# A gated recurrent layer on one core: VectorE's order within a step, and the x products dealt out anew

## The chip, the cores and the metric

The kernel runs on one core of a Trainium2 chip. The metric is the device time of one execution in microseconds (us). The kernel before took 1719.35 us, the median of three runs (1719.15 to 1720.79).

## The reference

The input x has 8 sequences of 512 steps with 512 features, all float32. A state h (8 x 512) starts from `cond_1024` and is carried through the steps:

```
fused = sigmoid(concat([x_t, h]) @ w_W + w_b)      # 1024 columns
r, z  = split(fused, 2)
m     = x_t @ wx_W + wx_b + r * (h @ wh_W + wh_b)
h_new = z * h + (1 - z) * tanh(m)
```

The output is x plus the sequence of the h_new. What depends on h alone must be done step after step; what depends on x (three products of 512 x 512 per step) can be done ahead.

## The kernel before, in words

**Layout.** Features stand on partitions. A step's products with h use h as the stationary operand (32 columns: four steps of 8 sequences, three of them zero) and weights as the moving one. TensorE is used as four column strips of 32: each product is four matmuls (j = 0 to 3, line 343) that write four groups of 32 partitions side by side. One such matmul shows as two records in the profile, so a product is 8 records. The result is transposed 32 x 32 by VectorE, so that features stand on partitions again.

**Halves and banks.** The state is in two halves, A (features of k = 0, 1) and B (k = 2, 3); the names in the profile say it (hTA, hTB, md0A, hd0B). The results of one step go to three PSUM tiles: bank A of 192 columns (h, z, r of half A), bank B of 128 (r, h of half B) and bank C of 64 (z of half B). "h" in this list is the product with `wh_W`.

**Order on TensorE** (line 32, loop at 337): A0 B0 A1 A2 A3 B1 B2 B3 C0 C1 C2 C3, a bank and the k of the state that it reads. A0 and A1 need the two quarters of the new half A, A2 and A3 those of the new half B. Behind the twelve come a few x products of later steps (lines 346 to 349). They are taken from a generator, `products` (line 289): for each eight steps (an octet, two groups of four) seven products in the manner of Winograd, each of two k and 192 columns, into four regions AL, DE, BE, GA of the PSUM tiles xp. That makes 14 products of one k, 56 matmuls. `take(later, 8 if s else 4)` takes one product in the first step of a group of four, and two in the others. From step 5 to step 500 there are such products; the first five steps do three larger, plain ones, and the last eleven none.

**The step on VectorE and ScalarE** (lines 420 to 445), written out by hand: the schedule is manual, so each engine runs its instructions in this order.
- `turn_r(0)`: VectorE transposes r of half A out of bank A (tr, line 371), ScalarE takes its sigmoid into md0A.
- `turn_h(0)`: VectorE transposes h into md1A (line 386).
- `turn_z(0)`: VectorE transposes z (tz, line 371); ScalarE takes the sigmoid of its negative into hd0A. A dependency made by hand (line 395) lets tz wait for r's sigmoid.
- `memory(0, q)` for the two quarters: a scan on VectorE (line 355) makes m = r * h + the x part from md0A and md1A; ScalarE takes tanh.
- `turn_r(1)`: the same for half B, out of bank B.
- `update(0, 0)`: a scan (line 355) makes the first quarter of the new half A, hTA.
- `turn_h(1)`, `turn_z(1)`, then `update(0, 1)`, which waits by hand for r's sigmoid of half B (line 429).
- `memory(1, q)`, `update(1, q)`: the same for half B.

Behind these come, spread over the octet (lines 444 to 501), ScalarE's copies of the new state, copies and additions that prepare PSUM and read the finished x products (lines 250 to 255 and 452 to 492), three small memsets on VectorE (line 499), and GpSimd's additions for the output (line 501) and for the x products (line 287). SyncE loads x and stores the output by chunks of 16 steps.

Of the kernel before, what the change touches and what calls it, by code (L numbers as in the profile page):

```python
# [14 lines left out]
NQ = 4  # L15
# [9 lines left out]
SYNC = mybir.DependencyInfo(mybir.DependencyClass.Sync, mybir.DependencyReason.DATA)  # L25
# [7 lines left out]
HALF = 192  # L33
# [8 lines left out]
def tile_cond_rnn_residual(  # L42
# [144 lines left out]
    def mm(out_, lhsT, rhs, start=False):  # L187
        nc.tensor.matmul(  # L188
            out_, lhsT, rhs, start=start, stop=False, skip_group_check=True
        )  # L190
# [23 lines left out]
    def act(key, out_, in_, func, **kw):  # L214
        inst = nc.scalar.activation(out_, in_, func, **kw).ins  # L215
        if key in written:
            tc.declare_no_dep(inst, written[key], reason="ordered through VectorE")
        written[key] = inst
        return inst
# [37 lines left out]
    def reg(r):  # L257
        return xps[r[0]][:, r[1]]

    def wx_of(kh, ch):  # L260
        return wx[:, 2 * kh : 2 * kh + 2, :, HALF * ch : HALF * ch + HALF]

    def x_half(o, n, kh):

        return x_of(o // 2, slice(2 * kh, 2 * kh + 2), 8 * (o % 2) + GS * n, GS)
# [23 lines left out]
    def products(o):  # L289

        t_ = [q[o % 2] for q in sx]
        for to, lhs, rhs in (
            (AL, x_half(o, 0, 0), wx_of(0, 0)),
            (DE, t_[0], tw[0]),
            (BE, t_[1], tw[1]),
            (AL, x_half(o, 0, 1), wx_of(1, 0)),
            (GA, t_[2], tw[2]),
            (BE, t_[3], wx_of(1, 1)),
            (GA, x_half(o, 1, 1), tw[3]),
        ):  # L300
            for k in range(2):
                for j in range(NQ):
                    mm(reg(to)[32 * j : 32 * j + 32], lhs[:, k], rhs[:, k, j])
                    yield

    def take(it, n=None):
        while n is None or n > 0:
            if next(it, it) is it:
                return
            n = None if n is None else n - 1  # L310

    def x_side():
        for o in range(2, NG // 2):
            yield from products(o)
# [4 lines left out]
    later = x_side()  # L319
# [8 lines left out]
    for i in range(T):  # L328
        g, s = divmod(i, GS)
# [7 lines left out]
        for n in (ORDER if i else FIRST).split():  # L337
# [3 lines left out]
            bank, k = n[0], int(n[1])  # L341
            hs = hT[k // 2][i % NH][:, :, k % 2, 2]
            for j in range(NQ):
                to = ps[bank] if i or bank != "A" else xps[0][:, XP["A"]]
                mm(to[32 * j : 32 * j + 32, :], hs, wh(bank, k, j))
        if i < 5:
            take(first[(i + 3) // 2], 2)
        else:
            take(later, 8 if s else 4)

        rows = slice(B * s, B * s + B)

        def scan(c_, out_, d0, d1):

            return nc.vector.tensor_tensor_scan(  # L355
                *[t_[:, :, c_].rearrange("p n c s -> p (n c s)") for t_ in (out_, d0, d1)],
                0.0,
                ALU.mult,
                ALU.add,
            ).ins  # L360
# [8 lines left out]
        def turned(n, hf):  # L369
            t_ = work.tile([P, 2, 32], F32, tag=f"t{n}{hf}", name=f"t{n}{hf}_{i}")  # L370
            inst = nc.vector.transpose(t_.rearrange("p c n -> p (c n)"), raw[n][hf]).ins  # L371
            return t_[:, :, rows], inst

        r_done = [None, None]

        def turn_r(hf):
            tr, _ = turned("r", hf)
            r_done[hf] = act(
                ("r", hf, g % 2, s),
                md0[hf][g % 2][:, rows, :, 1].rearrange("p n c -> p c n"),  # L380
                tr,
                AF.Sigmoid,
            )

        def turn_h(hf):
            inst = nc.vector.transpose(
                md1[hf][g % 2][:, :, :, 0].rearrange("p n c -> p c n"), raw["h"][hf]
            ).ins
            if hf == 0 and i + 1 - NH in pool_done:
                tc.add_manual_dep(inst, pool_done[i + 1 - NH].name, SYNC)  # L390

        def turn_z(hf):
            tz, inst = turned("z", hf)
            if hf == 0:
                tc.add_manual_dep(inst, r_done[0].name, SYNC)
            act(
                ("zc", hf, i % 2),
                hd0[hf][i % 2][:, :, :, 2].rearrange("p n c -> p c n"),
                tz,
                AF.Sigmoid,  # L400
                scale=-1.0,
            )
# [6 lines left out]
        def memory(hf, q):  # L409

            c_ = slice(q, q + 1)
            scan(c_, ms[hf], md0[hf][g % 2][:, rows], md1[hf][g % 2][:, rows])
            act(("n", hf, q, i % NH), state(hf, i, 1)[:, :, c_], ms[hf][:, :, c_, 1], AF.Tanh)

        def update(hf, q):
            s1 = (i + 1) % GS
            new = hT[hf][(i + 1) % NH][:, B * s1 : B * s1 + B]
            return scan(slice(q, q + 1), new, hd0[hf][i % 2], hT[hf][i % NH][:, rows])

        turn_r(0)  # L420
        turn_h(0)
        turn_z(0)
        memory(0, 0)
        memory(0, 1)
        turn_r(1)
        update(0, 0)
        turn_h(1)
        turn_z(1)
        tc.add_manual_dep(update(0, 1), r_done[1].name, SYNC)
        if i == 0:  # L430
# [169 lines left out]
```

## Time and profile before

| what | value |
|---|---|
| median of 3 runs | 1719.35 us |
| profiled execution | 1723.04 us, its span 1720.5 us |
| TensorE (PE), matmuls | 1698.3 us busy, 99% of the span |
| TensorE (PEld), weight loads | 1414.3 us busy, 82% |
| VectorE (DVE) | 1126.3 us busy, 65% |
| ScalarE (ACT) | 959.0 us busy, 56% |
| GpSimd (POOL) | 303.1 us busy, 18% |
| granted TensorE clock | 1.000 |

How to read it: matmuls are pipelined and their ends are modelled, so 99% does not say that TensorE works all the time; weight loads overlap the matmuls. The helpers record most instructions under one line each: all matmuls are line 188, all sigmoids, tanhs and state copies line 215, all scans line 355. The tiles tell them apart: out<-in. In a timeline the columns are the start (us from the span's start), the length from the first start to the last end, engine, line, operation, tiles and shapes, how many, and in brackets the engine's idle time before it with what ended it. In the waits view they are who waits, for whom, the total in us, how often, and the longest.

### The profile page before, as it was taken

To read this page: it belongs to the slowest core of one execution; us is meant where nothing else is said; L and a number is where in the kernel's file an instruction comes from. 1 tells how busy PE (TensorE), PEld (TensorE's weight loads), DVE (VectorE), ACT (ScalarE), POOL (GpSimd) and SP (SyncE) were. 2 spreads that over 40 slices of the span, in tenths; PEclk is the share of its full clock that TensorE was granted. 3 is DMA by queue.
4 is the path that set the end of the run, shared out by engine and by line. 5 is a ranking of instruction groups with operands and counts; after the bars stand their busy time and mean duration, and the time that the engine had idled before them with its cause. 6 is when DMAs were issued, how large, how long until landed. Compare 5 with 4: busy or idle time off the path is not lost.

```text
span 1720.5 us, 129875 instructions
## 1 busy us (share of the span) xinstructions
PE 1698.3 (99%) x56238; PEld 1414.3 (82%) x56238; DVE 1126.3 (65%) x9387; ACT 959.0 (56%) x5822; POOL 303.1 (18%) x1281
## 2 busy tenths in 40 slices
PE   9999999999999999999999999999999999999998
PEld 5888888888888888888888888888888888888886
DVE  5666666666666666666666666666666666666665
ACT  3555555555555555555555555555555555555554
POOL 1111111111111111111111111111111111111111
PEclk9999999999999999999999999999999999999999
DMA  4000000000000000000000000000000000000000
GB/s 174 17 5 17 17 17 17 17 5 17 17 17 17 5 17 17 17 17 5 17 17 17 18 11 11 17 17 17 17 5 17 17 18 17 5 17 11 11 11 10
DMA packets 11525, 31.40 MB, mean 18 GB/s; under 512 B 1220, under 2 KB 1732, under 8 KB 10824
## 3 DMA queue, kind: packets, MB, share of 16 engines
q1 hardware_dynamic: 10800, 22.94, 3.8%
q8 instruction: 440, 7.21, 1.7%
q14 instruction: 133, 1.09, 0.2%
q10 hardware_dynamic: 152, 0.16, 0.0%
HBM read 14.70 MB, written 8.39 MB: 13 GB/s over the span
## 4 chain that ended last, share of the span: by engine, by line
PE 88%; DVE 6%; ACT 4%; issue 1%; DMA 0%
PE A L188 42%; PE B L188 21%; PE xp L188 15%; PE C L188 10%; DVE tz L371 2%; DVE tr L371 2%; ACT md0A L215 2%; ACT hd0A L215 2%; DVE hTA L355 2%; ACT hTA L215 1%; DMA rows<-in_bias_dram 0%; DVE bias L203 0%; ACT hTB L215 0%; ACT xp L223 0%; DVE rows L120 0%
## 5 line engine op out<-in xcount | busy, mean ns | idle before, releaser
L188 PE MATMUL A<-wa,hTA 128*32 128x192 f32 x8176 | 527.3, 329 | 13.3 <-DVE hTA L355 4.0
L188 PE MATMUL A<-wa,hTB 128*32 128x192 f32 x8176 | 446.2, 335 | 0.2 <-DVE hTB L355 0.2
L188 PE MATMUL B<-wb,hTA 128*32 128x128 f32 x8192 | 414.0, 273 | 0.0
L501 POOL TENSOR_TENSOR ot<-xin,hTB 128x16 f32<-128x16 f32 x503 | 125.5, 250 | 1371.0 <-DVE hTB L355 1359.6
L371 DVE STREAM_TRANSPOSE tr<-A 128x64 f32<-128x64 f32 x511 | 127.9, 250 | 358.7 <-PE A L188 358.7
L188 PEld LDWEIGHTS A<-wa,hTB 128*32 128x32 f32 x8176 | 243.6, 125 | 111.5 <-DVE hTB L355 92.3
L188 PEld LDWEIGHTS B<-wb,hTA 128*32 128x32 f32 x8192 | 292.8, 121 | 40.9
L188 PEld LDWEIGHTS A<-wa,hTA 128*32 128x32 f32 x8176 | 236.2, 123 | 109.4 <-DVE hTA L355 61.6
L188 PE MATMUL B<-wb,hTB 128*32 128x128 f32 x8192 | 318.7, 273 | 0.0
L215 ACT ACTIVATE md0A<-tr 128x16 f32<-128x16 f32 x512 | 112.9, 221 | 318.2 <-DVE tr L371 318.2
L188 PEld LDWEIGHTS B<-wb,hTB 128*32 128x32 f32 x8192 | 241.4, 122 | 0.0
L355 DVE TENSOR_TENSOR_SCAN hTB<-hd0B,hTB 128x24 f32<-128x24 f32 x1024 | 158.1, 196 | 100.2 <-ACT hTB L215 100.0
L355 DVE TENSOR_TENSOR_SCAN hTA<-hd0A,hTA 128x24 f32<-128x24 f32 x1024 | 191.9, 187 | 43.1
L215 ACT ACTIVATE hd0B<-tz 128x16 f32<-128x16 f32 x512 | 115.7, 226 | 175.8 <-DVE tz L371 175.8
L188 PE MATMUL C<-wb,hTA 128*32 128x64 f32 x8192 | 209.4, 219 | 0.0
L188 PE MATMUL C<-wb,hTB 128*32 128x64 f32 x8192 | 209.3, 219 | 0.0
L215 ACT ACTIVATE hd0A<-tz 128x16 f32<-128x16 f32 x512 | 116.0, 227 | 162.0 <-DVE tz L371 162.0
L188 PEld LDWEIGHTS C<-wb,hTA 128*32 128x32 f32 x8192 | 186.9, 122 | 0.0
L371 DVE STREAM_TRANSPOSE tz<-A 128x64 f32<-128x64 f32 x511 | 128.0, 251 | 79.0 <-ACT md0A L215 75.9
L188 PE MATMUL xp<-tw,sx 128*32 128x192 f32 x2976 | 168.2, 326 | 0.1
L215 ACT ACTIVATE hTB<-hTB 128x16 f32<-128x16 f32 x512 | 121.8, 238 | 79.8 <-DVE hTB L355 75.5
L215 ACT ACTIVATE hTB<-m 128x8 f32<-128x8 f32 x1024 | 160.8, 206 | 0.0
(91 smaller groups left out, 2292.0 us busy)
## 6 DMA issues: line engine op xcount, KB each, us to landing
xin<-in_x_dram SPq DMA_DIRECT2D x31, 256.0 KB, 3.3
out_dram<-ot SPq DMA_DIRECT2D x31, 256.0 KB, 2.2
wx<-in_wx_dram SPq DMA_DIRECT2D x4, 768.0 KB, 7.1
wa<-in_wa_dram SPq DMA_DIRECT2D x4, 384.0 KB, 9.0
wb<-in_wb_dram SPq DMA_DIRECT2D x1, 1152.0 KB
wb<-in_wb_dram SPq DMA_DIRECT2D x1, 384.0 KB, 11.1
out_dram<-ot SPq DMA_DIRECT2D x1, 192.0 KB, 3.6
head<-in_xh_dram ACTq DMA_DIRECT2D x1, 144.0 KB, 5.1
```

The costliest lines, as they stand in the source:

```text
L188: nc.tensor.matmul(out_, lhsT, rhs, start=start, stop=False, skip_group_check=True)
L215: inst = nc.scalar.activation(out_, in_, func, **kw).ins
L355: return nc.vector.tensor_tensor_scan(*[t_[:, :, c_].rearrange("p n c s -> p (n c s)") for t_ in (out_, d0, d1)], 0.0, ALU.mult, ALU.add,).ins
L371: inst = nc.vector.transpose(t_.rearrange("p c n -> p (c n)"), raw[n][hf]).ins
L501: return engine.tensor_tensor(ot[:, t, 2 * hf : 2 * hf + 2, :].rearrange("p c n -> p n c"), x_of(c, slice(2 * hf, 2 * hf + 2), t, 1).rearr ...
```

## The change

Three things are edited.
1. tz of half A no longer waits by hand for r's sigmoid, but for the transpose of h ahead of it on VectorE. The wait for r's sigmoid is then with the scan that reads it.
2. On VectorE, the transpose of h of half B stands ahead of the first update of half A, no longer behind it.
3. Each step takes 8 matmuls from the generator. To make the number come out, 2 of the 14 products of one k in an octet are each done as two of 96 columns: 64 matmuls for eight steps. The x columns of four steps in a row, from the first of a group, were 192, 384, 384, 384; they are now 384, 384, 288, 288.

```diff
     def products(o):
...
-        for to, lhs, rhs in (
+        for n, (to, lhs, rhs) in enumerate((
             (AL, x_half(o, 0, 0), wx_of(0, 0)),
             (DE, t_[0], tw[0]),
             (BE, t_[1], tw[1]),
...
             (GA, t_[2], tw[2]),
             (BE, t_[3], wx_of(1, 1)),
             (GA, x_half(o, 1, 1), tw[3]),
-        ):
+        )):
             for k in range(2):
-                for j in range(NQ):
-                    mm(reg(to)[32 * j : 32 * j + 32], lhs[:, k], rhs[:, k, j])
-                    yield
+                w = HALF // 2 if (2 * n + k) % 7 == 3 else HALF
+                for c0 in range(0, HALF, w):
+                    for j in range(NQ):
+                        mm(
+                            reg(to)[32 * j : 32 * j + 32, c0 : c0 + w],
+                            lhs[:, k],
+                            rhs[:, k, j, c0 : c0 + w],
+                        )
+                        yield
...
-            take(later, 8 if s else 4)
+            take(later, 8)
...
         r_done = [None, None]
+        h_done = [None, None]
...
             inst = nc.vector.transpose(
                 md1[hf][g % 2][:, :, :, 0].rearrange("p n c -> p c n"), raw["h"][hf]
             ).ins
+            h_done[hf] = inst
...
             if hf == 0:
-                tc.add_manual_dep(inst, r_done[0].name, SYNC)
+                tc.add_manual_dep(inst, h_done[0].name, SYNC)
...
         turn_r(1)
+        turn_h(1)
         update(0, 0)
-        turn_h(1)
         turn_z(1)
```

## The prediction

> **What bounds the kernel now.** I read the chain of work that ended last, then the waits, then the timeline of single steps. By the chain's own engines the kernel looks bound by TensorE:
>
> ```profile
> PE 88%; DVE 6%; ACT 4%; issue 1%; DMA 0%
> ```
>
> The waits view speaks against that. TensorE's weight loads wait for VectorE's state of half B in nearly every step, and for half A in a quarter of them:
>
> ```profile
> PEld A L188 <- DVE hTB L355: 92.3, 499, 0.6
> DVE tz L371 <- ACT md0A L215: 76.0, 491, 0.2
> PEld A L188 <- DVE hTA L355: 61.6, 136, 0.6
> ```
>
> The test is a step with no x product. VectorE's timeline of such a step near the end, from its r transpose of half A to the next:
>
> ```profile
> 1698.71 0.25 DVE L371 STREAM_TRANSPOSE tr<-A 128x64 f32<-128x64 f32 x1 [0.76 <-PE A L188]
> 1698.89 0.21 DVE L386 STREAM_TRANSPOSE md1A<-A 128x64 f32<-128x64 f32 x1
> 1699.25 0.25 DVE L371 STREAM_TRANSPOSE tz<-A 128x64 f32<-128x64 f32 x1 [0.15 <-ACT md0A L215]
> 1699.42 0.23 DVE L355 TENSOR_TENSOR_SCAN m<-md0A,md1A 128x16 f32<-128x16 f32 x2
> 1699.57 0.23 DVE L371 STREAM_TRANSPOSE tr<-B 128x64 f32<-128x64 f32 x1
> 1699.88 0.21 DVE L355 TENSOR_TENSOR_SCAN hTA<-hd0A,hTA 128x24 f32<-128x24 f32 x1
> 1700.01 0.23 DVE L386 STREAM_TRANSPOSE md1B<-B 128x64 f32<-128x64 f32 x1
> 1700.15 0.21 DVE L371 STREAM_TRANSPOSE tz<-C 128x64 f32<-128x64 f32 x1
> ...
> 1700.81 0.31 DVE L355 TENSOR_TENSOR_SCAN hTB<-hd0B,hTB 128x24 f32<-128x24 f32 x2 [0.19 <-ACT hTB L215]
> ...
> 1702.01 0.25 DVE L371 STREAM_TRANSPOSE tr<-A 128x64 f32<-128x64 f32 x1 [0.76 <-PE A L188]
> ```
>
> It lasts 3.30 us. The 496 steps with x products go from the tr row at 39.55 to the one at 1682.20: 1642.65 / 496 = 3.31 us, the regular ones 3.306 (some 3 us sit in a few stragglers). Taking all x work away thus buys nothing: the period is that of a loop through VectorE. TensorE's and ScalarE's rows of the same step close it:
>
> ```profile
> 1700.14 0.55 PE L188 MATMUL A<-wa,hTA 128*32 128x192 f32 x8 [0.40 <-DVE hTA L355]
> 1700.73 0.51 PE L188 MATMUL A<-wa,hTA 128*32 128x192 f32 x8
> 1701.07 0.88 PE L188 MATMUL A<-wa,hTB 128*32 128x192 f32 x16
> ```
>
> ```profile
> 1698.99 0.22 ACT L215 ACTIVATE md0A<-tr 128x16 f32<-128x16 f32 x1 [0.80 <-DVE tr L371]
> 1699.53 0.22 ACT L215 ACTIVATE hd0A<-tz 128x16 f32<-128x16 f32 x1 [0.32 <-DVE tz L371]
> 1699.65 0.30 ACT L215 ACTIVATE hTA<-m 128x8 f32<-128x8 f32 x2
> ```
>
> The **B loop**: tr at 1698.71, first update of half B ends at 1700.81+0.21 = 1701.02, A2 starts at 1701.07 (2.36 after tr), next tr 0.94 later: 3.30. The **A loop**: the update ends at 1700.09, A0 starts at 1700.14 (1.43 after tr). A late A0 takes 0.59 to A1 (1700.14 to 1700.73); from there an early step, in which nothing waits, gives 0.33 to A2 and 0.90 from A2 to tr (27.82): 1.43+0.59+0.33+0.90 = 3.25. **TensorE's own** time comes from the same early step:
>
> ```profile
> 26.59 0.51 PE L188 MATMUL A<-wa,hTA 128*32 128x192 f32 x8
> 26.92 0.83 PE L188 MATMUL A<-wa,hTB 128*32 128x192 f32 x16
> ...
> 28.67 1.47 PE L188 MATMUL xp<-wx,xin 128*32 128x384 f32 x16
> ```
>
> A0 starts at 26.05 and x at 28.67: 2.62 for the twelve state products. One 192-column x product takes 0.325 (rows at 802.34, 802.66, 802.99), so steps with 384 columns need 3.27 and those with 192 need 2.95. The period is the largest of the three: 3.30, B, always.
>
> **The change, part by part.**
>
> *z transpose of half A (tz).* Its wait for r's sigmoid becomes a wait for h's transpose, which stands just ahead of it on VectorE. Behind it queue the A scans, tr of B and all that follows. Today tz starts 0.04 after the sigmoid's end (1698.99+0.22 = 1699.21, tz 1699.25). h ends at 1698.89+0.21 = 1699.10. No row shows VectorE waiting for itself. Bounds: tz at 1699.07 if the wait costs nothing beyond the engine's spacing (0.18, tr to h); at 1699.17 if it costs the 0.07 between the last A matmul's recorded end (801.42) and tr (801.49). I take 0.03 to 0.04, the usual step between VectorE and ScalarE: 1699.13, so 0.12 earlier, by the rows nearest in kind.
>
> *r's sigmoid at the scan.* It ends at 1699.21, the result is there by 1699.25; behind tz the scan issues at 1699.13+0.17 = 1699.30. The wait is covered by tz, with 0.05 to spare. The tanh then follows z's sigmoid by 0.12 as now, and m is ready in time (0.16 after the scan's start, against 0.40 to the tanh less the 0.17). So A's update moves 0.12 earlier: A0 can start 1.31 after tr, and the A loop is 3.13.
> The Trainium skill, "Perfetto Trace Analysis", section "Identifying Dependency Chains", speaks against this step: an instruction that waits for several engines may get a semaphore instruction ahead of it, and the scan now needs ScalarE's r and VectorE's h. The waits view shows the pattern of today, tz waiting for ScalarE and the scan for nobody; after, tz waits for h and the scan for r, so the rule should find one wait on each. By the rule the scan would be late by a price the page does not give.
> I bound such a price from rows: nothing, or 0.04 as for any handover; of this 0.04 would stay within the A loop, 3.17.
>
> *h of half B ahead of A's update.* It needs bank B, as tr of B ahead of it does. Moved up, it issues 0.17 after tr of B (now 1699.57, then 1699.45): 1699.62, and frees VectorE 0.13 later, at 1699.75. A's update is due at 1699.76. It fits in the hole of 0.31 that VectorE leaves today between 1699.57 and 1699.88. If that cover is short, A's update pays what is missing, up to 0.05. Behind the update nothing but tz of B stands: it starts at 1699.76+0.13 = 1699.89 instead of 1700.15 (bank C's last record ends at 1699.75, so it may start from 1699.82). All that follows in half B keeps its spacing, so B's update moves 0.26 earlier and the B loop is 3.04. Its r sigmoid follows A's tanhs on ScalarE as now.
>
> *The x products.* Columns by step of a group, from 192, 384, 384, 384 to 384, 384, 288, 288 (the same sum). Two of 14 products per eight steps become two of 96 columns. Bank C's 64 columns take 0.1125 (28.22 to 28.67 for four), 192 take 0.325; the line through both gives 0.166 for 96 and 0.006 for a split, 0.7 us for 62 octets times two. TensorE then needs 3.27 and 3.11.
> The Trainium skill, "TensorE: Matmul & The Clock Gate", section "Wait — 56ns, not 53.3ns?", puts a fixed 2.5 ns on each matmul; 8 more records per split would make an estimate of 2.5 us in all. I keep the 0.7 of the rows.
> Readers of the moved products: the second half of DE comes a step later, as does the first GA product of the last pair. ScalarE copies them a step or more behind: its tail begins 0.6 after the next A0, the products' results are there 0.25 after it. Nothing waits; if it did, ScalarE's tail would give up some of the 0.44 or more of idle time ahead of r's sigmoid. DMAs, SP's and POOL's queues are not touched; POOL's additions start earlier with B's update.
>
> **Sum.** Steps with 384 columns: the largest of 3.27 (TensorE), 3.13, 3.04, so 3.27. With 288: of 3.11, 3.13, 3.04, so 3.13. Mean 3.20. 496 × 3.20 = 1587.2, plus the 3 us of stragglers: 1590, against 1642.65, so 52.5 saved. The ten steps without x products (33.0 us) go at the A loop, 3.13: 1.7 saved. The first five were TensorE's already: nothing. In all 54. The profiled execution took 1723.0 for a span of 1720.5, the median of the runs is 1719.35; from the median, **1665 us** (the profiled span would be 1666).
>
> **Rivals.**
> 1. *TensorE and the A loop take turns* (the forecast, 0.78). For it: the two halves meet at nearly equal times, 3.11 and 3.13. Its own range: 1657 (tz at 1699.07, all steps at TensorE's 3.27 and 3.11, which is 1660, and the stragglers gone) to 1675 (tz at 1699.17: A loop 3.17).
> 2. *VectorE's wait for itself eats tz's gain* (0.13). If tz starts at 1699.25 as now, the A loop stays 3.25, steps with 288 columns last 3.25, the mean is 3.26: 1695. With half the gain it is 1680; with 0.08 more on the A loop, nearly the second wait (0.04) and the late h of B (0.05) together, 1685. Against it: h ends 0.11 before r's sigmoid does. For it: no row shows this wait.
> 3. *96 columns cost as much as 192* (0.03). Then every step takes 3.27: 1700. Against it: bank C's 64 columns with as many weight loads take a third of 192.
> 4. *Slower* (0.04): tz waits more than 0.21 after h's end, so that A's update, now with B's h ahead of it, passes 1699.94; from there the A loop exceeds 3.31 and sets every step. At 0.27 it is 3.37: 496 × 0.06 more, 1749. Against it: handovers in this trace cost 0.03 to 0.07.
> The remaining 0.02 are no change: all gains lost to a wait I do not see.
>
> **How the numbers follow.** What the measurement can tell from no change is about 0.2%, 3.4 us. Faster 0.94 (cases 1 to 3), same 0.02, slower 0.04. The range takes all of case 1 with 2 us of scatter between runs, and the better part of case 2: 1655 to 1686.
>
> **What would show it.** VectorE's tz should wait for no ScalarE row and start about 0.41 after tr (now 0.54); B's update 1.84 after tr (now 2.10); the waits of A's weight loads for hTB gone, those for hTA left in steps with 288 columns; periods alternating two by two, 3.27 and 3.13. I am wrong if tz starts at 0.5 or later, if A's update waits behind B's h, or if the product of 96 columns takes more than 0.17.

## The result, and the profile after

The changed kernel took 1674.33 us in the median of four runs (1671.65 to 1680.19), against 1719.25 us for the kernel before on the same chip: a ratio of 0.974, 95% interval 0.971 to 0.977. The forecast was 1665, the range 1655 to 1686. Measured twice more, on other occasions, the same program took 1702.64 and 1698.32 us (ratios 0.989, interval 0.987 to 0.990, and 0.986, interval 0.985 to 0.988), while the kernel before stayed at 1721. Both of these lie outside the range. The change makes the kernel faster each time, but by 1.1 to 2.6%, and the experiments had to find what sets the difference.

The profiled execution took 1671.65 us for a span of 1669.3. The chain of work that ended last, by engine, now lies on TensorE:

```profile
PE 97%; DMA 1%; DVE 1%; issue 0%; ACT 0%; SPq 0%
```

The waits of the changed kernel (who, for whom, total us, times, longest):

```profile
PEld A L188 <- DVE hTA L361: 22.4, 119, 0.4
PEld A L188 <- DVE hTB L361: 0.7, 2, 0.4
```

The wait for half B, 92.3 us in 499 steps before, is gone; that for half A is left in about half of the steps with 288 columns. VectorE's timeline of two steps (scans are now line 361, tr and tz line 377, h line 393):

```profile
802.44 0.25 DVE L377 STREAM_TRANSPOSE tr<-A 128x64 f32<-128x64 f32 x1 [0.60 <-PE A L188]
...
805.56 0.25 DVE L377 STREAM_TRANSPOSE tr<-A 128x64 f32<-128x64 f32 x1 [0.59 <-PE A L188]
805.74 0.21 DVE L393 STREAM_TRANSPOSE md1A<-A 128x64 f32<-128x64 f32 x1
805.98 0.25 DVE L377 STREAM_TRANSPOSE tz<-A 128x64 f32<-128x64 f32 x1
...
806.46 0.21 DVE L393 STREAM_TRANSPOSE md1B<-B 128x64 f32<-128x64 f32 x1
806.62 0.21 DVE L361 TENSOR_TENSOR_SCAN hTA<-hd0A,hTA 128x24 f32<-128x24 f32 x1
806.74 0.22 DVE L377 STREAM_TRANSPOSE tz<-C 128x64 f32<-128x64 f32 x1
...
807.42 0.31 DVE L361 TENSOR_TENSOR_SCAN hTB<-hd0B,hTB 128x24 f32<-128x24 f32 x2 [0.19 <-ACT hTB L215]
...
808.83 0.25 DVE L377 STREAM_TRANSPOSE tr<-A 128x64 f32<-128x64 f32 x1 [0.97 <-PE A L188]
```

The periods are 3.12 and 3.27. tz starts 0.42 after tr (0.54 before), 0.03 after h's end (805.74 + 0.21 = 805.95), so VectorE's wait for itself costs what a handover between engines costs. A's update comes 1.06 after tr (1.17 before), B's 1.86 (2.10). The medians of the steps from 13 to 499, by their place in a group of four, are 3.270, 3.270, 3.127, 3.125: mean 3.198, where the prediction had 3.20.

But the 496 steps with x products took 1595.4 us, 3.217 each. A regular step times 496 is 1586; the other 9 us sit in 42 steps that are 0.04 to 0.77 us longer than the median of their place (before: 2 us in 8 steps). These are called long steps below. TensorE's timeline in one of the longest:

```profile
972.75 0.40 PE L188 MATMUL C<-wb,hTB 128*32 128x64 f32 x15
973.72 0.22 PE L188 MATMUL C<-wb,hTB 128*32 128x64 f32 x1 [0.56 <-issue]
```

Fifteen matmul records of bank C, then nothing, then the sixteenth, whose operands had long been there: "issue" means that the profile knows nothing it waited for. From the page of the changed kernel, the busy times with the counts, and the queue that brings instructions:

```profile
PE 1655.0 (99%) x57230; PEld 1504.4 (90%) x57230; DVE 1102.7 (66%) x9387; ACT 956.9 (57%) x5822; POOL 300.5 (18%) x1281
...
q8 instruction: 448, 7.34, 1.8%
```

57230 matmul and 57230 weight-load records are 114460; divided by 448 packets that is 255.5 a packet, so one packet of 16 KB holds 256 of TensorE's instructions. Counted so from TensorE's first record, all nine gaps above 0.25 us in these steps (from the start of one matmul record to the start of the next) begin at the place 192 to 194 of a stretch of 256. This pointed to the supply of instructions, and the second half of the experiments is about it.

### The profile page after: what moved, and what is told of

Its sections match the earlier page's. It is cut to its first block, busy times and chain, and to the rows that moved or that the text cites. A ratio compares the mean times of both kernels' runs of the same rounds, so it can differ in the third digit from the quotient of the medians.

```text
span 1669.3 us, 131859 instructions
## 1 busy us (share of the span) xinstructions
PE 1655.0 (99%) x57230; PEld 1504.4 (90%) x57230; DVE 1102.7 (66%) x9387; ACT 956.9 (57%) x5822; POOL 300.5 (18%) x1281
## 4 chain that ended last, share of the span: by engine, by line
PE 97%; DMA 1%; DVE 1%; issue 0%; ACT 0%; SPq 0%
PE A L188 40%; PE B L188 26%; PE xp L188 18%; PE C L188 13%; DMA wb<-in_wb_dram 1%; DMA wx<-in_wx_dram 0%; DVE tr L377 0%; DVE tz L377 0%; DVE hTA L361 0%; DVE m L361 0%; DVE md1A L393 0%; DVE md1B L393 0%; ACT hTB L215 0%; ACT xp L223 0%; DVE hTB L361 0%
## 5 line engine op out<-in xcount | busy, mean ns | idle before, releaser
L188 PE MATMUL A<-wa,hTA 128*32 128x192 f32 x8176 | 536.1, 328 | 2.8 <-DVE hTA L361 2.8
L188 PE MATMUL A<-wa,hTB 128*32 128x192 f32 x8176 | 435.6, 326 | 0.1
L188 PE MATMUL B<-wb,hTA 128*32 128x128 f32 x8192 | 429.5, 273 | 0.8 <-DMA wb<-in_wb_dram 0.8
L188 PEld LDWEIGHTS B<-wb,hTA 128*32 128x32 f32 x8192 | 307.5, 122 | 37.6 <-DMA wb<-in_wb_dram 1.1
L188 PEld LDWEIGHTS A<-wa,hTB 128*32 128x32 f32 x8176 | 292.3, 122 | 45.7 <-DVE hTB L361 0.7
L188 PEld LDWEIGHTS A<-wa,hTA 128*32 128x32 f32 x8176 | 263.9, 123 | 37.5 <-DVE hTA L361 22.4
L188 PE MATMUL C<-wb,hTB 128*32 128x64 f32 x8192 | 218.6, 219 | 1.0 <-issue 1.0
L188 PE MATMUL C<-wb,hTA 128*32 128x64 f32 x8192 | 217.9, 219 | 0.0
L188 PE MATMUL xp<-tw,sx 128*32 128x192 f32 (+1 forms) x3472 | 186.1, 303 | 0.3 <-issue 0.2
L188 PEld LDWEIGHTS C<-wb,hTB 128*32 128x32 f32 x8192 | 167.2, 122 | 0.9 <-issue 0.8
```

The lines of the kernel that those rows point to most:

```text
L188: nc.tensor.matmul(out_, lhsT, rhs, start=start, stop=False, skip_group_check=True)
```

## The experiments

**Theory at first**: the period of a step is the longest of TensorE's own work, the loop through half A and the loop through half B. **Rival**: TensorE's busy share says it, and only the new deal of the x products counts. The first four kernels ran on one chip, where the kernel before took 1720.41. "Regular" is the median step by place in a group, "mean" the 496 steps divided by 496.

**1. VectorE's order alone (edits 1 and 2).** Against the changed kernel:

```diff
-                w = HALF // 2 if (2 * n + k) % 7 == 3 else HALF
+                w = HALF
...
-            take(later, 8)
+            take(later, 8 if s else 4)
```

> Edits 1 and 2 alone (VectorE's order), the x products as before: 192, 384, 384, 384 columns. Theory (the period of a step is the longest of TensorE's work, the A loop and the B loop): three steps of 3.27 us by TensorE, one of 3.13 by the A loop, mean 3.235 against 3.198 regular in the changed kernel; 496 x 0.037 = 18 us above it, less a little for fewer stragglers: 1687 to 1693. Rival (TensorE's busy share sets the time, so only the new deal of x products counts): 1719. Rival (the order alone gives all): 1674.

Measured: 1690.81 us (ratio 0.982, 0.981 to 0.984). Regular steps 3.123, 3.270, 3.270, 3.270. The order alone gives 30 us, where the whole change gave 45 in the first measurement, and the step with few x columns runs at the A loop, as expected.

**2. The new deal alone (edit 3).** Against the changed kernel:

```diff
-                tc.add_manual_dep(inst, h_done[0].name, SYNC)
+                tc.add_manual_dep(inst, r_done[0].name, SYNC)
...
-        turn_h(1)
         update(0, 0)
+        turn_h(1)
```

> Edit 3 alone (x columns 384, 384, 288, 288), VectorE's order as before. Theory: the B loop of 3.30 us sets every step whatever TensorE does, so 1719, plus or minus 2, and periods of 3.306 in all steps. Rival (the stalls of TensorE in the step with 192 columns are what is gained): steps of 3.27 and 3.25, mean 3.26, 1696, or down to 1665.

Measured: 1726.45 us (ratio 1.003, 1.001 to 1.004): slower than before. The regular steps are 3.307, 3.306, 3.303, 3.304, the B loop, wherever the columns lie; its waits show it:

```profile
PEld A L188 <- DVE hTB L361: 85.7, 453, 0.4
```

The rival falls. But the time is 6 us above the theory too: 11 us of long steps, against 2 before.

**3. Edits 1 and 3: h of half B stays behind A's update.**

```diff
-        turn_h(1)
         update(0, 0)
+        turn_h(1)
```

> Edits 1 and 3, but h of half B behind A's update as before. Theory: the A loop is 3.13 as in the changed kernel; the B loop gains only the 0.12 us of tz and is 3.18; steps 3.27 (TensorE) and 3.18 (B loop), mean 3.225: 496 x 0.027 = 13 above the changed kernel, 1687. TensorE's weight loads then wait for hTB in the steps with 288 columns. Rival (the place of h of half B is of no account): 1674.

Measured: 1701.73 us (ratio 0.989). Regular steps 3.270, 3.270, 3.186, 3.188, the predicted 3.27 and 3.18, and the 207 waits of the weight loads for half B are in the steps with 288 columns:

```profile
PEld A L188 <- DVE hTB L361: 41.3, 207, 0.4
```

The period is right, the time is not: 24 us lie in long steps.

**4. Edits 2 and 3: tz of half A waits for r's sigmoid.**

```diff
-                tc.add_manual_dep(inst, h_done[0].name, SYNC)
+                tc.add_manual_dep(inst, r_done[0].name, SYNC)
```

> Edits 2 and 3, but tz of half A waits for r's sigmoid as before. Theory: A loop 3.25 us as before, B loop 3.30 - 0.14 = 3.16; steps 3.27 (TensorE) and 3.25 (A loop), mean 3.26: 496 x 0.062 = 31 above the changed kernel, less some stragglers, 1700 to 1705. Rival (tz's wait is of no account, the B loop alone mattered): 1674 to 1680.

Measured: 1707.23 us (ratio 0.992). Regular steps 3.270, 3.270, 3.243, 3.242 (the A loop of 3.25), and no waits of note for half B; 15 us in long steps, and a time 2 us above the range expected.

So both parts of VectorE's order are needed, each for its own loop, and the regular periods of all four kernels came within 0.01 of the loops or of TensorE's 3.27. What the loops do not explain is the time in long steps: it differs from kernel to kernel, and it is what separates expectation from time in experiments 2 and 3. The next four ran together (before: 1720.91).

**5. The changed kernel again.**

> The changed kernel once more, to see the scatter of its times. Theory (its steps are fixed at 3.27 and 3.127 us, and what scatters is a few dozen stragglers, 9 us in the trace, where TensorE's instructions come late): regular periods the same to 0.002, stragglers between 5 and 15 us, times from 1670 to 1681.

Measured: 1702.64 us (1698.61 to 1704.11; ratio 0.989). Regular steps 3.271, 3.270, 3.127, 3.125 as in the first trace; but 41 us in 150 long steps instead of 9 in 42. My expectation of the scatter fails. The kernel before shows no such change, nor does the granted clock (1.000). The waits of its weight loads, and the longest gap:

```profile
PEld A L188 <- DVE hTA L361: 16.8, 86, 0.4
PEld xp L188 <- issue: 15.9, 50, 0.7
PEld C L188 <- issue: 13.1, 37, 1.0
```

```profile
1282.13 0.24 PEld L188 LDWEIGHTS C<-wb,hTB 128*32 128x32 f32 x11
1283.38 0.13 PEld L188 LDWEIGHTS C<-wb,hTB 128*32 128x32 f32 x2 [1.00 <-issue]
```

The gap is again inside a run of like instructions that wait for nothing. Sixty gaps of TensorE exceed 0.25 us here, and all sixty begin at place 192 or just behind it of 256 instructions.

**6. More instructions for the same columns.**

```diff
-                w = HALF // 2 if (2 * n + k) % 7 == 3 else HALF
+                w = HALF // 2
...
-            take(later, 8)
+            take(later, 16 if s < 2 else 12)
```

> The changed kernel with all 14 x products of an octet as two of 96 columns, the columns of each step kept (384, 384, 288, 288). Theory: 0.006 us for each of 12 more splits, so regular steps of 3.283 and 3.127, mean 3.205, 3 us more; and 11% more TensorE instructions make them late more often, so stragglers grow from 9 to 15 or 25 us: 1683 to 1693. Rival (a fixed 2.5 ns for each matmul record, one after the other): regular steps of 3.31 and 3.15, 15 us more from these alone. Rival (instructions cost nothing): 1675 to 1677.

Measured: 1868.16 us (ratio 1.086, 1.084 to 1.088), far above every expectation. From its page, and from the waits of its weight loads:

```profile
PE 1762.0 (94%) x63182; PEld 1626.4 (87%) x63182; DVE 1126.2 (60%) x9387; ACT 965.4 (52%) x5822; POOL 303.1 (16%) x1281
...
q8 instruction: 494, 8.09, 1.9%
```

```profile
PEld xp L188 <- issue: 50.4, 120, 1.7
PEld C L188 <- issue: 48.7, 109, 0.9
PEld B L188 <- issue: 48.5, 107, 1.3
PEld A L188 <- issue: 37.2, 86, 1.0
```

TensorE waits for its own instructions in every bank, 344 gaps above 0.25 us, all at place 192 or just behind it. The four waits add up to 185 us, nine tenths of the 202 us by which the 496 steps exceed 3.205 each. The narrow products themselves are not dear where no gap falls. In TensorE's timeline a row of 16 records is two of them, and the next row starts 0.33 us later, where one product of 192 columns takes 0.325:

```profile
801.92 0.53 PE L188 MATMUL xp<-tw,sx 128*32 128x96 f32 x16
802.25 0.53 PE L188 MATMUL xp<-wx,xin 128*32 128x96 f32 x16
802.58 0.33 PE L188 MATMUL A<-wa,hTA 128*32 128x192 f32 x1
```

The mean step is 3.613 us for 62 matmuls of 4 instructions: 248, or 14.6 ns an instruction, 3.73 us for 256. The kernel of experiment 5 gives the same: 3.282 us for 224 is 14.65 ns, 3.75 us for 256. **New theory**: TensorE's instructions come in pieces of 256, and a piece takes at least some 3.7 us; whatever asks for more is held to this pace.

**7. No x products (their part of the computation is left out).**

```diff
-            take(later, 8)
+            pass
```

> The changed kernel without the x products from step 5 on (this part of the computation is left out), all else kept. Theory: TensorE needs 2.62 us, so the A loop of 3.127 sets all steps; 496 x 3.127 = 1551, plus 77 outside of them, and TensorE with 0.5 us of idle time a step and 14% fewer instructions has few stragglers, 0 to 3 us: 1628 to 1632. Rival (stragglers come from elsewhere, such as ScalarE or the DMAs of x): 9 us of them stay, 1637. Rival (TensorE's own time sets the steps): below 1560.

Measured: 1626.60 us, 1.4 below the range expected. Every regular step is 3.124, the A loop, with not one long step. The page's queue and the waits:

```profile
q8 instruction: 385, 6.31, 1.7%
```

```profile
PEld A L188 <- DVE hTA L361: 218.2, 507, 0.4
```

192 instructions in 3.124 us are 4.17 us for 256, slower than the supply can do; the loads wait for half A alone. That the A loop is where the sum put it (3.13) is shown here without TensorE's work on top; of the B loop this shows only that it is no longer than that.

**8. tz of half A with no wait by hand.**

```diff
-            if hf == 0:
-                tc.add_manual_dep(inst, h_done[0].name, SYNC)
```

> The changed kernel with no wait by hand on tz of half A. The scan then has two waits, for VectorE's h and ScalarE's r, and an extra semaphore instruction carries one of them. Theory: tz starts 0.35 us after tr instead of 0.42, the A loop falls below TensorE's 3.11, steps with 288 columns go from 3.127 to 3.11, 4 us less: 1670; if the extra instruction costs 0.04 the A loop is 3.10 and the time the same within 1 us. Rival (a second wait is dear, 0.1 or more): steps with 288 columns of 3.16 or longer, 1682 or more.

Measured: 1701.89 us, no different from the 1702.64 beside it. VectorE's timeline of a step with 288 columns:

```profile
709.98 0.25 DVE L377 STREAM_TRANSPOSE tr<-A 128x64 f32<-128x64 f32 x1 [1.12 <-PE A L188]
710.15 0.21 DVE L393 STREAM_TRANSPOSE md1A<-A 128x64 f32<-128x64 f32 x1
710.28 0.21 DVE L377 STREAM_TRANSPOSE tz<-A 128x64 f32<-128x64 f32 x1
710.51 0.28 DVE L361 TENSOR_TENSOR_SCAN m<-md0A,md1A 128x16 f32<-128x16 f32 x2
...
713.09 0.25 DVE L377 STREAM_TRANSPOSE tr<-A 128x64 f32<-128x64 f32 x1 [0.62 <-PE A L188]
```

tz starts 0.30 after tr (0.42 with the wait), the scan 0.53 (0.59), and the step is 3.11, TensorE's own time: the loops were shortened as expected, and a second wait on the scan costs nothing that these rows show. "Perfetto Trace Analysis", section "Identifying Dependency Chains", of the Trainium skill has it that an instruction which waits for several engines may get a semaphore instruction ahead of it; this kernel has one per step ahead of the scan (515 of them on VectorE at the scans' line, 3 in the changed kernel), and the scan starts 0.03 after the recorded end of r's sigmoid (710.48). The time lies where the rival had it, at 1682 or more, but the step is not the 3.16 of the rival, and the changed kernel beside it takes as long. The 4 us expected do not show: at the pace of experiment 5, 224 instructions need 3.28 us, whatever the loops ask for.

**Rival to the new theory**: narrow products are dear in themselves, by weight loads or a fixed cost. The last four ran together (before: 1721.08).

**9. The changed kernel a third time.**

> The changed kernel a third time, beside three others on the same chip. New theory (TensorE gets its instructions in pieces of 256 at no less than some 3.67 to 3.74 us a piece, 14.3 to 14.6 ns an instruction, and this differs from chip to chip): 224 instructions a step need 3.21 to 3.28 us, against 3.198 that the loops and TensorE's work ask for, so the time is set by the supply: 1674 to 1704, more than half of its long TensorE gaps again at place 192 of 256. Rival (one measurement was a fluke): back at 1670 to 1681.

Measured: 1698.32 us; mean step 3.272, 3.74 us for 256 instructions; 47 of 47 gaps above 0.25 us at place 192 or just behind it.

**10. VectorE's order alone, beside it.** The kernel of experiment 1.

> VectorE's order alone (edits 1 and 2), x columns 192, 384, 384, 384, on the same chip as the changed kernel. New theory: 220 instructions a step need 3.15 to 3.22 us, less than the 3.233 its loops ask for, so it hardly moves from chip to chip: 1685 to 1693. On a chip where the changed kernel takes 1700 it is the faster of the two, where that takes 1674 the slower. Rival (the deal in halves is a gain everywhere): 15 or more above the changed kernel.

Measured: 1687.01 us (ratio 0.980, 0.979 to 0.982), 11 us less than the changed kernel on the same chip. 220 instructions a step need 3.21 us at 14.6 ns, and its loops ask for 3.233, so it has few long steps (5 us).

**11. The order alone with a free tz.** Experiment 10 with the edit of experiment 8.

> The order alone, and tz of half A with no wait by hand; x columns as before. The A loop is 3.08 in the run with a free tz, so steps are 3.08 and three of 3.27, mean 3.222, 5 us below the order alone: 1680 to 1688. At the slowest supply seen (14.6 ns, 3.22 us for 220) it gains 2 to 3.

Measured: 1681.21 us (ratio 0.978, 0.976 to 0.979), the fastest on this chip. Its step with 192 columns, which was 3.123 with the wait, from tr to tr:

```profile
1003.28 0.25 DVE L377 STREAM_TRANSPOSE tr<-A 128x64 f32<-128x64 f32 x1 [1.02 <-PE A L188]
...
1006.36 0.25 DVE L377 STREAM_TRANSPOSE tr<-A 128x64 f32<-128x64 f32 x1 [0.82 <-PE A L188]
```

Here the shorter A loop pays, 3.08, since the supply leaves it room. It is ahead of both kernels on this chip; beside the changed kernel where that took 1674.33 it was not run.

**12. As many instructions, a third of the x columns (the other two thirds are left out).** Experiment 6 with:

```diff
-                            reg(to)[32 * j : 32 * j + 32, c0 : c0 + w],
+                            reg(to)[32 * j : 32 * j + 32, c0 : c0 + 32],
                             lhs[:, k],
-                            rhs[:, k, j, c0 : c0 + w],
+                            rhs[:, k, j, c0 : c0 + 32],
```

> The kernel of the halves with each x product narrowed from 96 to 32 columns (two thirds of the x columns are left out): the same 248 instructions a step, but TensorE's own work falls from 3.20 to some 2.85 us a step. Theory of the supply: the time stays where the halves were, 3.55 to 3.65 us a step, 1840 to 1890. Rival (narrow products are dear by their columns, their weight loads or their fixed cost, not by the fetching of instructions): steps of 3.13 to 3.3, 1630 to 1700.

Measured: 1862.94 us, 5 less than with all columns (experiment 6, on another chip). The mean step is 3.600 us, 3.72 for 256 instructions. Its page and waits:

```profile
PE 1683.4 (90%) x63182; PEld 1474.6 (79%) x63182; DVE 1125.7 (60%) x9387; ACT 966.0 (52%) x5822; POOL 303.0 (16%) x1281
...
q8 instruction: 494, 8.09, 1.8%
```

```profile
PEld xp L188 <- issue: 75.1, 126, 1.0
PEld C L188 <- issue: 69.9, 116, 1.2
```

Two thirds of the x columns less, and the time stays: the columns are not what costs. A fixed cost of each matmul or weight load is not excluded by this run, whose counts are those of experiment 6; against it stand the rows there, with 0.33 us for two narrow products and the lost time in gaps at one place of 256. Together they leave the number of instructions, and the rival falls.

## Why the prediction was right, and where it was off

| kernel | instructions a step | regular mean, us | mean, us | us for 256 | time, us |
|---|---|---|---|---|---|
| no x products | 192 | 3.124 | 3.124 | 4.17 | 1626.60 |
| before | 220 | 3.308 | 3.312 | 3.85 | 1719.35 |
| order alone (exp. 1, 10) | 220 | 3.233 | 3.253, 3.243 | 3.79, 3.77 | 1690.81, 1687.01 |
| deal alone (exp. 2) | 224 | 3.305 | 3.327 | 3.80 | 1726.45 |
| tz and deal (exp. 3) | 224 | 3.228 | 3.277 | 3.74 | 1701.73 |
| h of half B and deal (exp. 4) | 224 | 3.256 | 3.286 | 3.76 | 1707.23 |
| order, free tz | 220 | 3.222 | 3.232 | 3.76 | 1681.21 |
| changed, first | 224 | 3.198 | 3.217 | 3.68 | 1674.33 |
| changed, again and third | 224 | 3.198, 3.198 | 3.282, 3.272 | 3.75, 3.74 | 1702.64, 1698.32 |
| all halves | 248 | none | 3.613 | 3.73 | 1868.16 |
| all halves, 32 columns | 248 | none | 3.600 | 3.72 | 1862.94 |

Instructions are 4 per matmul of the program (two matmul records and two weight loads), without the few semaphore instructions. The last two asked for 3.21 and less; most of their steps are longer than the loops ask for, so no regular mean is given. Experiments 1 to 4 ran on an occasion of their own; there experiment 3, whose loops and TensorE's work ask for 3.69 us for 256, took 3.74.

- **What bounds the kernel**: right. The B loop of 3.30 set every step before (experiment 2), and TensorE's 99% were no evidence.
- **tz**: predicted 0.12 earlier, measured 0.12; the wait of VectorE for itself is 0.03. Left alone as before, it sets the A loop at 3.24 (experiment 4).
- **h of half B ahead of A's update**: covered by the hole as said; A's update comes at 1.06 after tr (1.05 predicted), B's at 1.86 (1.84). Left behind, it sets the B loop at 3.19 (experiment 3).
- **The x products**: right in TensorE's time (3.27, and 3.11 in experiment 8; a product of 96 columns takes 0.165, put at 0.166), wrong in the price. I had 0.7 us for the splits, which TensorE's rows bear out (two of 0.165 for one of 0.325, 124 times: 0.6), and an estimate of 2.5 us by a fixed cost per matmul. What the sum lacks is the four more matmuls of a split, 16 instructions: four a step on average, 0.058 us at 14.6 ns, 29 us in 496 steps wherever the supply sets the pace. It hardly does so in the first trace (3.68 us for 256) and does in the other two.
- **The sum**: its failing term is "plus the 3 us of stragglers". I took them for noise that stays. They were the first sign of the supply, which the slack of the B loop covered: 3.85 us for 256 instructions before. With 3.198 a step the changed kernel asks for 3.65. The term measured 9 us in the first trace and 41 in the second: with it the forecast is 1671 and 1703. None of my rivals had this; "all gains lost to a wait I do not see" was given 0.02, and on the second occasion 18 of the 54 us forecast were left. That the first measurement fell inside the range is therefore in part the luck of the occasion: the loops were forecast rightly, and the supply, which the sum does not have, happened to be nearly fast enough. A further 2 us of the gain of the first trace lie ahead of step 5, which starts at 37.67 us instead of 39.55. With the changed kernel it started at 37.63 to 40.14 in three traces, so these 2 us cannot be put down to the change.

Two things stay open. Why a piece takes 3.7 us is shown in part only. In the median of the stops of experiment 6, the instruction behind the stop starts 2.59 us after the start of the instruction queue's last packet, and the packet itself takes 1.11 of them; the next packet starts 1.14 us after that instruction. Together this is 3.73 us, the pace of the table, so the packets come one at a time. What passes between a packet's end and the instruction, and before the next packet, is not shown. And why the first measurement was faster than the others is not known. The traces differ in the packets' median time, 0.98 us in the first trace of the changed kernel against 1.13 and 1.10 in the later two, but whether this is the cause, and whether it is the chip's or the hour's, cannot be told from four occasions.

## What to carry to other kernels

Work out for each candidate of the bound what the period would be alone, and test it on a stretch of the same trace where one of them is missing; a busy share of 99% and a chain of 88% on TensorE were both compatible with TensorE not being the bound. Then count the instructions of the engine that becomes the bound: with many short matmuls, divide the time by their number, and treat gaps that end with "issue" as a resource near its limit, not as noise. A split that balances the columns is paid in instructions, and may cost more than the imbalance: on the chip of experiments 9 and 10 the new deal cost 11 us.

## What the runs showed of the hardware

- TensorE's instructions were fetched all through the execution, one 16 KB packet for 256, and the pace was bounded at 3.72 to 3.75 us a packet over long stretches (14.5 to 14.65 ns an instruction) on three occasions (experiments 3, 5, 6, 9 and 12), and 3.68 or less on one. When a piece was late, TensorE stopped at the same place of the 256, whatever stood there.
- A wait of VectorE for its own transpose cost 0.03 us from its recorded end, as a wait for ScalarE does; without it the next transpose starts 0.13 after the one before, while that is still running.
